# Four PSUM banks in turn for the pieces of a visit, and smaller steps for the work between

## The chip, the cores and the metric

The kernel runs on one core of a Trainium2 chip. The metric is device time in microseconds for one execution, from the median of ten runs. Everything is in float32.

## The reference

The input x has two images of 256 channels and 56 x 56 places, so 3136 tokens an image. The first layer is a linear attention over places (a convolution of 1 x 1 on each side, batch normalisation, relu, and x added). The second layer works on tokens:

```
t = to_tokens(x)                                   # (2, 3136, 256)
t = t + softmax_causal(q k^T / 8) v @ W_proj       # 4 heads of 64, on layernorm(t)
# mixture of experts, on n = layernorm(t):
probs = softmax(n @ gate_w + gate_b)               # 8 experts
cw    = the two largest probs of a token, else 0
t = t + sum_e cw[:, e] * (gelu(n @ W1[e] + b1[e]) @ W2[e] + b2[e])
```

W1 is 256 x 512 for each expert, W2 512 x 256. The kernel computes only the two chosen experts of a token, so each image's tokens have to be sorted by expert before the experts can start on them.

## The kernel before, in words

**Stages.** The first layer takes the first 100 us. Then comes the attention of image ("batch") 0, then of batch 1, from about 108 to 868 us, then the experts, in 105 blocks of 128 rows, 3.73 us of TensorE a block. Batch 0 is sorted while batch 1's attention runs, batch 1 while the first 42 blocks of the experts run, which hold batch 0's rows alone.

**Attention.** `attend` (L631) goes through seven tiles i of 448 queries. For each tile and each pair of heads hp (two), it goes through the key chunks j of 128: 4, 7, 11, 14, 18, 21 and 25 of them, so 200 steps a batch. A step is `scores` (L668, four 64 x 64 quadrants of TensorE at once, into a tile of two PSUM banks), the exponential on ACT (L676), for the chunks that the diagonal cuts a mask on DVE (L678), and the row sums on DVE (L690). `values` (L708) follows three steps later (`LAG`, L777). A key chunk is whole when no query of the tile is ahead of it, and cut otherwise; each pair of heads has four or five cut chunks, which alternate with whole ones at the end of its steps.

**PSUM.** All eight banks are in use: pool `pm` (L465) has two single banks, `psc` (L1869) two tiles of two banks for the scores, `py` one tile of two banks for the values. `bank` (L469) hands out those of `pm`. Every piece of work between the steps takes its bank from there: the projections of queries and keys (`query_key`, L550, copied out by ACT at L558), of values (`value`, L565, copied at L574), the transposes of normalised tokens (L536, copied at L542), the output projection (`project_out`, L618, added by DVE at L623), and the sums over keys (`sum_rows`, L732, copied at L737).

**Visits.** After the last step of a pair of heads comes a `visit` (L1913), 28 in all. It issues the projections that a later tile needs (`ahead`, L1875): four pieces for queries and keys or values, and one or two transposes; the last visits of batch 0 do this for batch 1, and in the last tile of batch 1 there are none. Then `sum_rows` runs. Between the steps, `between` (L1924) is called once for each step.

**The queue.** Other work lies in generators in a `queue`: `tokens(b)` (L1784), which runs `project_out`, then `dispatch`, and for batch 0 the loads of W1 (`w1s`) and of the first expert rows (`early_rows`). A generator gives True when a portion is done, False when it has to wait, and "pe" when TensorE work is next. `pull(n)` (L1757) goes through the queue from its front until n portions are done; a generator that gave False lets the next one have its turn, one that gave True ends the search. One that gave "pe" is held until `products` (L1772), called twice in a visit, lets it go on. Before the change, `between` calls `pull(2)` at every second step, and each visit calls `pull()` twice:

```python
                        for _ in range(2):
                            pull()
                            products()
```

`project_out` (L608) works in pairs of token chunks: for each chunk the product over two halves of 128 channels into one bank, the addition, for batch 0 a store to `rest_d`, and then for the pair the mean and variance of each chunk (`stats`, L173: `bn_stats` L177 and `bn_aggr` L178). After that it gives True once for batch 0, three times for batch 1.

**Sorting.** `dispatch` (L951) computes the inverse deviation of all tokens with four Newton steps on DVE, the gate's softmax, the two experts and the place of each token; nearly all are DVE operations on 25 to 200 elements a partition. Behind most of them stands `yield from op()`, which for batch 0 gives True once or twice in turn. At its end the rows are scattered: for each of the 25 chunks DVE writes a normalised copy `xr` (L1302) and POOL issues two indirect DMAs to `x_slots` (L1310). For batch 0 the copies take turns in two buffers, and a chunk gives True and then False.

**Experts.** At block n the program first fetches the rows of three blocks (one group) up to n + 6 ahead on SP (`fetch`, L1332, DMA L1350), loads groups up to n + 3 (`load`, L1368), then does the products of block n, the transposes of blocks n + 1 or n + 2, and `meanwhile` (L1997), which pulls two portions of the queue, three while batch 1 is being sorted. Group 14 is the first with rows of batch 1. Its fetch at block 36 calls `need` (L1977), which pulls until all of batch 1's rows have been sent:

```python
                def need(b):
                    while not sent[b]:
                        pull(every=True)
```

SP runs its queue in order, so the stores of results (L1466) that come after a fetch wait behind it.

The engines' instruction order is the program's order in these stages.

Of the kernel before, what the change touches and what calls it, by code (L numbers as in the profile page):

```python
# [10 lines left out]
F32 = mybir.dt.float32  # L11
# [17 lines left out]
def conv_attn_moe_kernel(  # L29
# [52 lines left out]
    P = 128  # L82
# [9 lines left out]
    NCH = -(-N // P)  # L92
    W = 448
# [79 lines left out]
    def stats(b, n, m, k, pool, nm):  # L173

        for a in range(m):
            st6 = pool.tile([P, 6], F32, tag="st6", name=f"st6_{nm}_{n}_{a}")
            nc.vector.bn_stats(st6[:k], ts[b][:k, n + a, :C])  # L177
            nc.vector.bn_aggr(ts[b][:k, n + a, MEAN : MEAN + 2], st6[:k])  # L178
# [9 lines left out]
    with tc.tile_pool(name="c_w", bufs=1) as cw, tc.tile_pool(name="c_s", bufs=2) as cs, tc.tile_pool(  # L188
        name="c_big", bufs=5, space=PSUM
# [169 lines left out]
        first = fold(0, gram(0, iter(())))  # L359
# [99 lines left out]
    def layer1(nm, general):  # L459

        with ExitStack() as whole:
# [4 lines left out]
            bg = pool(whole, "bg", bufs=2)  # L466
            g1 = pool(whole, "g1", bufs=1)

            def bank(name, shape=(P, 512)):  # L469
                return pm.tile(list(shape), F32, tag="m", name=f"{name}_{nm}")  # L470

            def centre_gate(place):
# [135 lines left out]
            def project_out(b, qT, done):  # L608

                for first, m, k in pairs():  # L610
                    while done() < (first + m - 1) * P + k:
                        yield False
                    yield "pe"
                    for n in range(first, first + m):
                        o = n * P
                        ps = bank(f"pp_{b}_{n}")
                        for c in range(NH):
                            nc.tensor.matmul(  # L618
                                ps[:k, : C + E], qT[:, c, o : o + k], wpr[:, c, :],
                                start=(c == 0), stop=(c == NH - 1),  # L620
                            )
                        t = ts[b][:k, n, : C + E]
                        nc.vector.tensor_tensor(t, t, ps[:k, : C + E], ALU.add)  # L623
                        if b == 0:
                            nc.sync.dma_start(out=rest_d[:k, n], in_=t[:, :C])
                    stats(b, first, m, k, bg, f"o{nm}{b}")

                    for _ in range(3 if b else 1):
                        yield True

            def attend(  # L631
                b, qT, kT, v, fst, fs, psc, py, visit, between, clock, later, finished
# [4 lines left out]
                steps, firsts = [], {}  # L637
                for i in range(NB):
                    nk = -(-((i + 1) * W) // P)
                    whole_js = [j for j in range(nk) if (j + 1) * P - 1 <= i * W]  # L640
                    cut = [j for j in range(nk) if j not in whole_js]
# [136 lines left out]
                for n in range(len(steps) + LAG):  # L778
                    if 0 < n <= len(steps) and steps[n - 1][4]:
                        i, hp = steps[n - 1][:2]  # L780
                        visit(i, hp)
                        sum_rows(hp, i)
                    if n < len(steps):
                        i = steps[n][0]
                        between(i, ends[i] - n)

                    late = n >= LAG and steps[n - LAG][3]
                    if n >= LAG:
                        due(clock[0])
                        clock[0] += 1  # L790
                    if n >= LAG and not late:
                        values(n - LAG)
                    if n < len(steps):
                        scores(n)
                    if late:
                        values(n - LAG)
# [154 lines left out]
            def dispatch(b):  # L951

                t = ts[b]
                tail = chunk(NCH - 1)
                ops = [0]

                def small_piece():

                    if b:
                        yield True  # L960
# [5 lines left out]

                def op():

                    ops[0] += 1
                    for _ in range(0 if b else 1 + ops[0] % 2):  # L970
                        yield True

                def small(name, last=E, dt=F32):
# [2 lines left out]
                def wide(ap):  # L976
# [8 lines left out]
                    small(k, 1).rearrange("p t o -> p (t o)") for k in ("newton_x", "newton_y", "red")  # L985
                )
                nc.vector.tensor_scalar(x, var, 1e-5, None, ALU.add)
                nc.vector.tensor_scalar(
                    y.bitcast(I32), x.bitcast(I32), 1, None, ALU.arith_shift_right
                )  # L990
                nc.vector.tensor_scalar(
                    y.bitcast(I32), y.bitcast(I32), -1.0, float(0x5F3759DF), ALU.mult, ALU.add
                )
                yield from small_piece()
                for i in range(4):
                    to = var if i == 3 else y
                    nc.vector.tensor_tensor(z, y, y, ALU.mult)
                    nc.vector.tensor_tensor(z, z, x, ALU.mult)
                    nc.vector.tensor_scalar(z, z, -0.5, 1.5, ALU.mult, ALU.add)
                    nc.vector.tensor_tensor(to, y, z, ALU.mult)  # L1000
                    yield from op()
                    yield from small_piece()
# [294 lines left out]
                for n in range(NCH):  # L1297
                    kk = chunk(n)
                    xr = (scatter_rows[0] if b else bg).tile(
                        [P, width], F32, tag="xr", name=f"xr_{nm}{b}_{n}"  # L1300
                    )
                    nc.vector.tensor_scalar(  # L1302
                        xr[:kk, :C], t[:kk, n, :C],
                        t[:kk, n, MEAN : MEAN + 1], t[:kk, n, RSTD : RSTD + 1],
                        ALU.subtract, ALU.mult,
                    )
                    if b:
                        nc.vector.tensor_copy(xr[:kk, C:], t[:kk, n, C + E - 2 : SLOT + 1])  # L1308
                    for k in range(2):
                        s = nc.gpsimd.indirect_dma_start(  # L1310
                            out=xds[b],
                            out_offset=bass.IndirectOffsetOnAxis(ap=idxs[b][:kk, k, n : n + 1], axis=0),
                            in_=xr[:kk],
                            in_offset=None,
                            bounds_check=xds[b].shape[0] - 1,
                            oob_is_err=False,
                        )
                        group = f"x_slots_{nm}{b}"
                        tc.declare_no_dep(s.ins, group=group, reason="different rows")
                        tc.add_to_no_dep_group(group, s.ins)  # L1320
                        if b or k:
                            yield True
                    if b == 0:
                        yield False
                sent[b] = True

            def experts(w1s, w2s, b2s, ex, es, ps6, between, need, written, settle, decide):
# [538 lines left out]
            else:  # L1866
                fst = pool(att, "fst", bufs=5)
                fs = pool(end, "fs", bufs=2, side="right")
                psc = pool(att, "psc", bufs=2, space=PSUM)  # L1869
                py = pool(att, "py", bufs=1, space=PSUM)  # L1870
                projections = [project_qkv(b, qT, kT, v, px) for b in range(B)]
                finished = [[0] * NH for b in range(B)]
# [2 lines left out]
                def ahead(b, i, hp):  # L1875

                    xs, qks, vs = projections[b]
                    if i + 1 < NS:
                        if hp == 0:
                            return qks(i + 1), xs(i + 2)[:1]  # L1880
                        return vs(i + 1), xs(i + 2)[1:]
                    if b + 1 == B:
                        return [], []
                    xs, qks, vs = projections[b + 1]
                    if hp == 0:
                        return [], xs(0)
                    return qks(0) + vs(0), xs(1)
# [22 lines left out]
                for b in range(B):  # L1910
                    queue.append(tokens(b, qT, lambda b=b: min(finished[b])))

                    def visit(i, hp):  # L1913

                        now, then = ahead(b, i, hp)
                        for piece in now:
                            piece()
                        for _ in range(2):
                            pull()
                            products()  # L1920
                        for piece in then:
                            piece()

                    def between(i, left):  # L1924
                        if b == B - 1 and i == NB - 1:

                            now = load_w2(left < NCH - 4)
                            for _ in range(1 if left > NCH - 4 else 2):
                                next(now, None)

                        tick[0] += 1
                        if tick[0] % 2:
                            pull(2)

                    due = attend(
                        b, qT, kT, v, fst, fs, psc, py, visit, between,
                        clock, later, finished[b],
                    )
# [250 lines left out]
```

## Time and profile before

| | |
|---|---|
| median of 10 runs | 1320.39 us (1318.14 to 1324.05) |
| the profiled execution | 1321.51 us, span 1319.8 us |
| matmuls of scores (L668), 3184 records | 339.4 us busy |
| matmuls of values (L708), 3184 records | 339.9 us busy |
| exponentials (L676), 400 | 331.0 us on ACT |
| row sums (L690), 372 | 379.9 us on DVE |
| first hidden product of the experts (L1432) | 205.8 us busy in all 102 blocks |
| DMA | 124.49 MB, mean 94 GB/s |

Busy time of an engine is the time in which at least one of its instructions ran. Matmuls are pipelined and their ends are modelled. In the waits, a row names the engine, the tile that the waiting instruction writes and its line, then what released it, then the total in us, how often, and the longest. In the timeline a row is the start, the length, the engine, the line and the operation; the brackets hold the idle time before it and what ended that.

### The profile page before, as it was taken

The page shows a single profiled execution, that of the slowest core. Times are in us where ns is not written, and L with a number is a line of the kernel's source. Part 1 is how long each engine was busy: PE and PEld are TensorE (multiplying, and loading weights), DVE is VectorE, ACT ScalarE, POOL GpSimd, SP SyncE. Part 2 cuts the span into 40 slices and gives each one's busy share as a digit, 9 for nine tenths or more (in the row PEclk, how much of TensorE's full clock was granted, in tenths as well). Part 3 has the DMA queues.
Part 4 walks back from the last instruction along what each step waited for, and adds up shares of the span by engine and source line. Part 5 has one row for each costly group of instructions (what it writes and reads, how often), then busy time and mean ns, then how long its engine had stood idle before and what let it go on. Part 6 is the DMA issues. An engine that isn't in the chain of part 4 may idle for free. (4 is left out here: it accounts for less than half of the span.)

```text
span 1319.8 us, 28094 instructions
## 1 busy us (share of the span) xinstructions
PE 1268.9 (96%) x10589; PEld 825.6 (63%) x10589; DVE 796.0 (60%) x1665; ACT 610.6 (46%) x1228; POOL 347.7 (26%) x317
## 2 busy tenths in 40 slices
PE   8999999999999999999999999999998999899997
PEld 7875445544444445444444444579987899799996
DVE  1582667567777744766877777764753443355654
ACT  0154565555666554555555556543422333234432
POOL 1103330000002223310116630000066312655551
PEclk9999999999999999999999999999999999899999
DMA  9994100000000001000002233321234333466654
GB/s 306 384 349 133 31 11 30 24 9 25 9 16 9 25 1 26 23 16 9 14 18 81 81 140 96 104 73 54 68 129 146 118 113 98 139 190 193 196 158 128
DMA packets 111182, 124.49 MB, mean 94 GB/s; under 512 B 19686, under 2 KB 100823, under 8 KB 111040
## 3 DMA queue, kind: packets, MB, share of 16 engines
q1 hardware_dynamic: 97216, 93.44, 23.2%
q0 software_dynamic: 9840, 25.67, 5.8%
q10 hardware_dynamic: 3984, 3.50, 0.9%
q8 instruction: 87, 1.43, 0.5%
q14 instruction: 55, 0.45, 0.1%
HBM read 62.71 MB, written 61.05 MB: 94 GB/s over the span
## 5 line engine op out<-in xcount | busy, mean ns | idle before, releaser
L676 ACT ACTIVATE st_f<-sc_f 128x896 f32<-128x896 f32 (+5 forms) x400 | 331.0, 841 | 222.7 <-PE sc_f L668 194.5
L690 DVE TENSOR_TENSOR acc_f<-acc_f,st_f 128x896 f32<-128x896 f32 (+5 forms) x372 | 379.9, 1021 | 71.3 <-ACT st_f L676 59.8
L668 PE MATMUL sc_f<-qT_f,kT_f 64*64 64x448 f32 (+6 forms) x3184 | 339.4, 500 | 6.4 <-ACT st_f L676 3.4
L708 PE MATMUL yp_f<-st_f,v_f 64*64 64x448 f32 (+6 forms) x3184 | 339.9, 501 | 5.3 <-DVE st_f L678 4.2
L1441 ACT ACTIVATE g_f<-ht_f,b1b 128x128 f32<-128x128 f32 x408 | 117.0, 372 | 251.9 <-PE ht_f L1432 137.4
L668 PEld LDWEIGHTS sc_f<-qT_f,kT_f 64*64 64x64 f32 x3184 | 119.3, 133 | 162.3 <-issue 124.4
L708 PEld LDWEIGHTS yp_f<-st_f,v_f 64*64 64x64 f32 x3184 | 117.9, 133 | 159.3 <-issue 134.0
L1432 PE MATMUL ht_f<-xT_f,w_f 128*128 128x128 f32 x1632 | 205.8, 279 | 6.4 <-issue 5.3
L1432 PEld LDWEIGHTS ht_f<-xT_f,w_f 128*128 128x128 f32 x1632 | 201.4, 195 | 13.2 <-issue 7.9
L720 POOL TENSOR_TENSOR qT_f<-both_f 128x448 f32<-128x448 f32 x28 | 36.9, 1318 | 502.3 <-ACT both_f L719 502.3
L1310 POOL DMA_INDIRECT x_slots<-xr_f,idx x100 | 110.0, 1100 | 142.8 <-DVE xr_f L1308 98.9
L1420 DVE COPY w_f<-w1s_f 128x1024 f32 x102 | 72.2, 710 | 91.5 <-PE ht_f L1432 40.3
L521 POOL TENSOR_SCALAR xn_f<-t 128x256 f32<-128x256 f32 (+1 forms) x50 | 80.9, 1626 | 158.5 <-PE xp_f L536 66.2
L1472 POOL DMA_INDIRECT y_tokens<-ys_f,to_f x57 | 57.8, 1015 | 126.8 <-DVE ys_f L1461 103.1
L550 PE MATMUL qk_f<-px_f,wat 128*128 128x512 f32 (+2 forms) x224 | 88.3, 546 | 0.4 <-ACT px_f L542 0.4
L1461 DVE TENSOR_TENSOR ys_f<-yp_f,kT_f 128x128 f32<-128x128 f32 x102 | 29.6, 290 | 96.5 <-PE yp_f L1451 71.7
L550 PEld LDWEIGHTS qk_f<-px_f,wat 128*128 128x128 f32 x224 | 40.5, 190 | 45.6 <-issue 41.1
L686 DVE COPY acc_f<-st_f 128x896 f32<-128x896 f32 x28 | 17.9, 641 | 79.9 <-ACT st_f L676 76.1
L1451 PE MATMUL yp_f<-px_f,g_f 128*128 x204 | 62.6, 387 | 3.1 <-issue 3.1
L1451 PE MATMUL yp_f<-v_f,g_f 128*128 x204 | 62.0, 384 | 2.3 <-issue 2.3
L678 DVE TENSOR_TENSOR st_f<-st_f,keep 128x256 f32<-128x256 f32 (+1 forms) x112 | 45.7, 408 | 29.7 <-ACT st_f L676 29.7
L1451 PE MATMUL yp_f<-kT_f,g_f 128*128 x204 | 62.1, 385 | 0.9 <-issue 0.6
(274 smaller groups left out, 1269.3 us busy)
## 6 DMA issues: line engine op xcount, KB each, us to landing
x_slots<-fill SPq DMA_DIRECT2D x1, 8190.0 KB
xb_f<-x_slots SPq DMA_DIRECT2D x60, 130.0 KB
x_slots<-fill SPq DMA_DIRECT2D x1, 7296.0 KB
y_slots<-ys_f SPq DMA_DIRECT2D x57, 128.0 KB
kept<-t SPq DMA_DIRECT2D x2, 3200.0 KB
x<-in_x_dram SPq DMA_DIRECT2D x14, 448.0 KB
rb_f<-inverses SPq DMA_DIRECT2D x56, 112.0 KB
xr<-in_x_rows_dram SPq DMA_DIRECT2D x12, 512.0 KB
```

The source lines that it names most:

```text
L521: nc.gpsimd.tensor_scalar(xn[:k, a], ts[b][:k, n + a, :C], ts[b][:k, n + a, MEAN : MEAN + 1], ts[b][:k, n + a, RSTD : RSTD + 1], ALU.subtr ...
L550: nc.tensor.matmul(ps[:, :w], wat[:, c, d0 : d0 + P], px[:, s % 2, c, :w], start=(c == 0), stop=(c == NH - 1),)
L668: nc.tensor.matmul(ps[h : h + HS, a, c0:W], kT[hp][rows, j * P + h : j * P + h + HS], qT[rows, hp, q0 + c0 : q0 + W], start=True, stop=True,)
L676: nc.scalar.activation(st[:k, :, c0:], ps[:k, :, c0:W], AF.Exp, scale=SCALE)
L690: nc.vector.tensor_tensor(acc[:k, :, c0:], acc[:k, :, c0:], st[:k, :, c0:], ALU.add)
L708: nc.tensor.matmul(yp[a * HS : (a + 1) * HS, h // HS, c0:W], v[hp][h : h + HS, j, a, :HS], st[h : h + HS, a, c0:], start=first, stop=bool( ...
L1310: s = nc.gpsimd.indirect_dma_start(out=xds[b], out_offset=bass.IndirectOffsetOnAxis(ap=idxs[b][:kk, k, n : n + 1], axis=0), in_=xr[:kk], i ...
L1420: nc.vector.tensor_copy(w, w1s[:, :, bass.ds(e, 1), :].rearrange("p c e h -> p c (e h)"))
L1432: nc.tensor.matmul(ht[:, k, :], w[:, c, k * P : (k + 1) * P], xT[:, c, :], start=(c == 0), stop=(c == NH - 1),)
L1441: nc.scalar.activation(g[:, k, :], ht[:, k, :], AF.Gelu, bias=b1bs[b][:, k, i : i + 1])
L1451: nc.tensor.matmul(yp[:, :C], g[:, k, :], w2s[k][:, bass.ds(e, 1), :].rearrange("p e d -> p (e d)"), start=(k == 0), stop=(k == KH - 1),)
L1472: s = nc.gpsimd.indirect_dma_start(out=y_tokens, out_offset=bass.IndirectOffsetOnAxis(ap=to[:, n % GB : n % GB + 1], axis=0), in_=ys, in_o ...
```

## The change

The change has four parts.

1. During a visit `bank` goes round four places: the two banks of `pm`, then the two halves of a tile of `psc`, taken as a score tile would be. A new score tile is taken at every third place of the round. `sum_rows` after the visit, and work pulled in `between`, use `pm` alone, as before.
2. For batch 0 `project_out` no longer computes the variances in the visit. It puts a generator `closer` at the front of the queue, which does one chunk a portion, and goes straight on to the next pair. `dispatch` of batch 0 starts when all 25 are closed.
3. For batch 0 every operation of the sorting, those of the Newton steps too, is now a portion of its own (`op` gives True once), and a scattered chunk gives True twice instead of True and False.
4. Visits do not pull any more. `between` pulls one portion at each step, except at the cut steps of the first tile, which has no others.

```diff
+            ring, score_banks = [], []
+
             def bank(name, shape=(P, 512)):
+                turn = ring[0] % 4 if ring else 0
+                if turn > 1:
+                    if turn == 2:
+                        ring[1] = score_banks[0].tile([P, 2, 512], F32, tag="sc", name=f"{name}_{nm}")
+                    ring[0] += 1
+                    flat = ring[1][:, turn - 2]
+                    if shape[2:]:
+                        return flat[:, : shape[1] * shape[2]].rearrange("p (a w) -> p a w", a=shape[1])
+                    return flat[:, : shape[1]]
+                if ring:
+                    ring[0] += 1
                 return pm.tile(list(shape), F32, tag="m", name=f"{name}_{nm}")
...
                         if b == 0:
                             nc.sync.dma_start(out=rest_d[:k, n], in_=t[:, :C])
+                    if b == 0:
+                        queue.appendleft(closer(b, first, m, k))
+                        continue
                     stats(b, first, m, k, bg, f"o{nm}{b}")
 
-                    for _ in range(3 if b else 1):
+                    for _ in range(3):
                         yield True
+                while b == 0 and unclosed[0]:
+                    yield False
+
+            unclosed = [NCH]
+
+            def closer(b, first, m, k):
+
+                for n in range(first, first + m):
+                    stats(b, n, 1, k, bg, f"o{nm}{b}")
+                    unclosed[0] -= 1
+                    yield True
...
-                        between(i, ends[i] - n)
+                        between(i, ends[i] - n, (steps[n][2] + 1) * P > i * W + 1)
...
                 def op():
 
-                    ops[0] += 1
-                    for _ in range(0 if b else 1 + ops[0] % 2):
+                    if b == 0:
                         yield True
...
                 for i in range(4):
                     to = var if i == 3 else y
                     nc.vector.tensor_tensor(z, y, y, ALU.mult)
+                    yield from op()
                     nc.vector.tensor_tensor(z, z, x, ALU.mult)
+                    yield from op()
                     nc.vector.tensor_scalar(z, z, -0.5, 1.5, ALU.mult, ALU.add)
+                    yield from op()
                     nc.vector.tensor_tensor(to, y, z, ALU.mult)
                     yield from op()
...
                     if b == 0:
-                        yield False
+                        yield True
                 sent[b] = True
...
                 psc = pool(att, "psc", bufs=2, space=PSUM)
+                score_banks.append(psc)
...
                         now, then = ahead(b, i, hp)
+                        ring[:] = [0, None]
                         for piece in now:
                             piece()
                         for _ in range(2):
-                            pull()
                             products()
                         for piece in then:
                             piece()
-
-                    def between(i, left):
+                        ring.clear()
+
+                    def between(i, left, cut):
...
                         tick[0] += 1
-                        if tick[0] % 2:
-                            pull(2)
+                        if not cut or i:
+                            pull()
```

Three more `yield from op()` stand behind the three operations ahead of the Newton loop.

More of the change, by code (lines that the diff above doesn't have):

```diff
@@ L954, in dispatch @@
                 tail = chunk(NCH - 1)
-                ops = [0]
                 def small_piece():
@@ L997, in dispatch @@
                     nc.vector.tensor_tensor(z, y, y, ALU.mult)
+                    yield from op()
                     nc.vector.tensor_tensor(z, z, x, ALU.mult)
+                    yield from op()
                     nc.vector.tensor_scalar(z, z, -0.5, 1.5, ALU.mult, ALU.add)
+                    yield from op()
                     nc.vector.tensor_tensor(to, y, z, ALU.mult)
```

## The prediction

> **What bounds the kernel now.** I read the busy shares and the clock row first, then busy time by stretches of the span, then the waits of TensorE inside the attention, then two rows of the timeline.
>
> ```profile
> PE 1268.9 (96%) x10589; PEld 825.6 (63%) x10589; DVE 796.0 (60%) x1665; ACT 610.6 (46%) x1228; POOL 347.7 (26%) x317
> ```
>
> TensorE is busy 96% of the span, and the other engines hang on it. A change can only give back its gaps, so the question is in which stretch they lie and what ends them. By stretches (columns: length, then busy time of PE, PEld, DVE, ACT, POOL, granted clock, DMA share, GB/s):
>
> ```profile
> 108.00:545.00 437.00, 430.06 (x4093) 205.98 (x4094) 279.61 (x422) 242.29 (x377) 81.13 (x52) 1.00 0.08 20
> 545.00:685.00 140.00, 134.96 (x1322) 62.05 (x1325) 101.25 (x192) 78.68 (x119) 20.52 (x13) 1.00 0.05 10
> 685.00:775.00 90.00, 82.95 (x842) 35.97 (x844) 67.55 (x103) 45.43 (x63) 60.82 (x52) 1.00 0.28 92
> ```
>
> These three are nearly the whole attention: up to 545 plain attention, 545 to 685 with the first batch's sorting between its steps, 685 to 775 with its scatter. PE is idle for 6.9, 5.0 and 7.1 us. The expert stage splits at the second batch's scatter:
>
> ```profile
> 868.00:956.00 88.00, 86.69 (x585) 79.82 (x582) 52.04 (x163) 35.14 (x112) 1.36 (x1) 1.00 0.24 72
> 956.00:1040.00 84.00, 74.17 (x458) 66.17 (x456) 37.79 (x148) 23.80 (x85) 51.48 (x50) 0.94 0.39 128
> ```
>
> From 956 to 1040 POOL issues 50 indirect DMAs, PE is idle 9.8 us and the clock falls to 0.94. What PE waited for in the attention (108 to 870):
>
> ```profile
> PE yp_f L708 <- DVE st_f L678: 4.2, 7, 1.1
> PE sc_f L668 <- ACT st_f L676: 3.4, 5, 1.2
> PE xp_f L536 <- DVE t L623: 2.2, 6, 1.1
> PE sp_f L732 <- DVE t L623: 1.9, 3, 0.7
> PE sp_f L732 <- ACT kT_f L558: 1.8, 7, 0.4
> ...
> PE sp_f L732 <- ACT v_f L574: 0.9, 3, 0.3
> ...
> PE pp_f L618 <- DVE t L623: 0.6, 1, 0.6
> ```
>
> Each sp, xp and pp row is a visit's piece that wants one of two PSUM banks whose last reader, a copy on ACT or an add on DVE, is not done: the wait that four banks should remove. The first two rows are the steps' own chain, in which the sorting's operations stand on DVE. Last, when batch 1's rows are out: the final scatter and the first fetch behind it on SP.
>
> ```profile
> 1036.03 1.12 POOL L1310 DMA_INDIRECT x_slots<-xr_f,idx  x1 [0.30 <-issue]
> ```
> ```profile
> 1038.95 1.44 SPq L1350 DMA_DIRECT2D xb_f<-x_slots  x3
> ```
>
> **The banks.** A visit with four pieces, a transpose and sum_rows asks for six banks. Of two, sum_rows takes the one that the last-but-one piece has just filled. Of four, it takes one filled five pieces earlier. The rows above plus ACT px 0.4 and DVE L585 0.2 are 5.2 us for sp, 2.2 for xp and 0.6 for pp: 8.0. Of these the two visits of batch 1's last tile stay: there one pair takes turns 0 and 1 and sum_rows comes back to turn 0, 0.57 us each. That leaves 6.9. The upper end is the weight loads' idle time before the same instructions: 16.2 us at L732 (6.2, 5.2, 3.4, 1.2, 0.2), and about 4 at L536 and L618, so 20; part of it lies under matmuls that still stream. I take 8, near PE's own rows. New waits, with the other pieces, the scores and so ACT's exponentials queued behind them on PE: the first borrowed bank, third in a visit, must be left by the exponential two steps back; in the visit at 431 it was left as the visit began (431.47), two bank times of 0.89 before it is wanted. The second borrowed pair is wanted at the seventh bank, 5 us on. Scores after the visit wait for copies of 0.59 us, emptied several pieces earlier except where the transpose itself is the borrowed one: 0 to 3 us, taken at 0. Its cover is the score buffer's idleness in a visit; without it each of 28 visits would pay one 0.59 copy, 16 us.
>
> **The variances.** 25 chunks of 0.41 (L177) plus 0.18 (L178) are 14.8 us of DVE, moved out of the visits, one chunk per step. A full step is 1.5 us of PE and 1.09 of DVE (L690), so a 0.59 is 0.18 too much for it; four in a row lag 0.7 us, which five st buffers cover and later steps recover. Price 0. In the short tiles (7 to 11 steps) the cover may fail: 0.7 in 6 visits, 4 us. The rest_d stores keep their place on SP.
>
> **The sorting.** Yields of batch 0's dispatch: before, 42 op() calls at 1.5 each plus 20 others, 83; after, 57 plus 20, 77. But pulls fall too: before, one per step on average and two in each visit; now one per step and none in visits. I walked both step lists: its first operation moves from visit i=1, hp=1 of batch 1 to step 23, its first scatter from step 94 to 100, its last from 138 to 148 (of 200). The w1 loads follow at 150 to 164 and the first expert rows at 166 to 169, behind nothing on SP but that scatter and ahead of step 200 by 30 steps, 45 us: hidden. Past POOL's queue the scatter moves beside one more sum L720 of 1.3 us. DVE no longer meets Newton in bursts of four, and no extra chunk falls into a visit, where DVE stood 5.4 us for L1302 on the two xr buffers. PE's idle rows here are 2.3 (545 to 685, L678) and 5.8 (685 to 775: sc 2.2, yp 1.9, sc issue 1.7). I take 2 of these 8.1 as gained. Ends: 5 gained; or 4 lost, since at a tile's end eight steps with masks need about 9.4 us of PE and 8.7 of DVE, and eight operations of 0.3 instead of five make DVE late by 0.8 in five tiles.
>
> **What the order does to batch 1.** While dispatch always yields True, and the scatter now too, tokens(1) behind it in the queue is never reached. Before, the scatter's False let it through: pairs 2, 4 and 6 of its projection ran in visits at 709, 750 and 788. Now these three wait, 3 x 1.78 = 5.3 us of PE (a pair is eight records of L618, 0.222 apart), which leave the attention and come back in the experts: zero in sum. Behind them its sorting starts at block 17 instead of 12, its scatter at block 25 instead of 20. Block 36 forces what is left, since fetch(14) needs all rows: one chunk of 25 before, eight now. DVE takes 8 x 0.58 = 4.6 us of it, within the two blocks by which weights run ahead. POOL is the bound: 0.98 plus 0.30 idle is 1.28 per DMA, 62.7 us from first to last, 76.8 in this trace because of gaps. Five blocks of 3.73 move the first from 959.26 to 977.9 (without the stalls, which fall later then). The end is 1040.6 at full rate, 1054.7 with all the old gaps, and 1046 with two gaps of 2.8, which I take. SP then issues 2.9 later, as above; behind it stand the y_slots stores of blocks 33 on. From SP's issue to block 42's transposes at 1049.50 were 10.6, of which I take 5 as slack: the addition L1386 (0.96) ran at 1045.07 behind other DVE work, and only 5.6 are needed. So the transposes come at 1049, 1055 or 1063: 0, 5 or 14 us lost. A gain is excluded, since the same POOL work starts later. I take 5.
>
> The stalls of this stretch went with a clock of 0.94. [...]
>
> **Sum.** The profiled execution took 1321.51 us (span 1319.8), 1.1 over the median of 1320.39. 1321.5 - 8 (banks) - 2 (sorting) + 5 (batch 1) = 1316.5, and 1315.4 against the median. I forecast 1315.5. Own range: bank gain 7 to 12, sorting -5 to +2, batch 1 0 to 9, which together rarely reach their ends: 1307 to 1321.
>
> **The rivals.**
> - *Slower: the second batch's scatter decides.* Place: SP's fetch L1350 at block 36, with PE idle at block 40. Price 14 for the late rows, and 5 for a slow clock as from 1137 to 1160 (23 us at 0.78, 0.22 x 23), less 10 gained: 1329. It decides once the last scatter comes 15 us later than now. For it: POOL is fed only 1.5 chunks a block; against: at full rate it ends within 5 us of before.
> - *DVE takes the waits over.* Gain 6 at the banks, 4 lost at the masks, 4 at batch 1: 1322. For it: L678 is already the longest wait; against: DVE is busy 72% from 545 to 685.
> - *Everything hides.* Banks 14, sorting 4, batch 1 nothing: 1302.
> - *The change doesn't do what it says.* If a borrowed tile's halves are waited for together, the second half waits for the copy of the first, 0.59 plus 0.2, in some 24 visits: 19 lost, no bank gain, 1342. No row shows a tile used so.
>
> **How the numbers follow.** Forecast 0.58, scatter 0.16, DVE 0.14, hides 0.08, not as said 0.04. About 0.2%, 2.6 us, is what a measurement here can tell from no change. Of the forecast 0.52 is faster by more and 0.06 within; hides is faster; DVE gives 0.02 faster, 0.09 same, 0.03 slower; scatter 0.02 same and 0.14 slower. Faster 0.62, same 0.17, slower 0.21. The range leaves out the last case, most of hides and the tail of scatter: 1304 to 1328.
>
> **What would show it.** Right: rows of sp, xp and pp on L558, L574 and L623 nearly gone in the attention; clock 1.00 there; the attention ends some 15 us earlier (10 gained, 5 of moved matmuls); batch 1's first scatter near 968 (977.9 less 10) instead of 959; SP's L1350 behind it and a PE gap at block 40. Wrong: new waits of PE on L558 or L574 at pieces or scores, more than 10 us on L678, or no gap at block 40.

## The result and the profile after

The changed kernel takes 1351.12 us (median of 9 runs, 1347.71 to 1354.62) beside 1320.75 for the kernel before (31 runs, 1314.83 to 1324.87). The ratio is 1.0232, 95% interval 1.0216 to 1.0248: 30 us slower, where 5 us faster was forecast, and beyond the range's upper end of 1328. The profiled execution took 1347.96 us, its span is 1346.2, so 26.4 us over the span of before. The change adds lines, so those of after lie higher: matmuls of queries and keys L563 (L550 before), of values L578 (L565), their copies L571 and L587 (L558, L574), the second batch's scatter L1341 (L1310), the fetch behind it L1381 (L1350), the expert blocks' transposes L1440 (L1409).

The page first. TensorE is busy about as long as before (1271.7 us, 1268.9 before), in a longer span:

```profile
PE 1271.7 (94%) x10589; PEld 823.4 (61%) x10589; DVE 792.1 (59%) x1665; ACT 607.7 (45%) x1228; POOL 352.5 (26%) x317
```

The stretches of the span (columns as in the table of before) say where:

```profile
108.00:545.00 437.00, 420.88 (x3983) 198.68 (x3985) 267.88 (x400) 234.03 (x363) 76.14 (x49) 1.00 0.08 20
545.00:685.00 140.00, 135.54 (x1342) 62.36 (x1334) 101.07 (x195) 78.52 (x123) 24.91 (x15) 1.00 0.05 12
685.00:775.00 90.00, 84.05 (x840) 36.92 (x840) 64.06 (x96) 48.08 (x69) 45.05 (x37) 1.00 0.17 55
...
1000.00:1100.00 100.00, 75.69 (x483) 67.44 (x482) 38.60 (x142) 25.23 (x90) 47.24 (x46) 0.88 0.38 119
```

Up to 545, TensorE is now idle for 16.1 us instead of 6.9, in the plain attention where the banks were to help. In 545 to 775 the idle time is 10.4 instead of 12.1. And from 1000 to 1100 it is idle 24.3 us at a clock of 0.88.

**First loss: the attention.** The first expert block starts at 880.14 us instead of 869.65, although three pairs of projections, 5.3 us of TensorE, left the attention. What TensorE waited for from 108 to 871 (us in total, times, longest):

```profile
PE qk_f L563 <- ACT kT_f L571: 8.8, 13, 1.2
PE v_f L578 <- ACT v_f L587: 4.8, 9, 0.5
PE sc_f L695 <- ACT st_f L703: 4.0, 5, 1.2
PE pp_f L631 <- DVE t L636: 2.6, 5, 0.5
PE v_f L549 <- ACT v_f L587: 2.2, 2, 1.6
...
PE yp_f L735 <- DVE st_f L705: 0.4, 1, 0.4
```

Against the waits of before, the rows of qk_f and v_f are new (the one at L549 is a transpose into the second half). The old ones did shrink: the rows of sp_f add up to 2.5 instead of 5.2, and the first row of before, values behind the mask on VectorE (L678, now L705), fell from 4.2 to 0.4. What the new rows are is seen in the first visit (timeline: start, duration, engine, line and operation; in brackets the idle time before it and what ended it):

```profile
113.03 5.42 PE L563 MATMUL qk_f<-px_f,wat 128*128 128x512 f32 x12
...
118.48 0.58 ACT L571 COPY kT_f<-qk_f 128x512 f32<-128x512 f32 x1 [1.13 <-PE qk_f L563]
...
119.12 1.98 PE L563 MATMUL qk_f<-px_f,wat 128*128 128x512 f32 x4 [0.68 <-ACT kT_f L571]
```

Three pieces run on without a gap: twelve matmuls. The third is the first half of the borrowed tile. ScalarE copies it from 118.48 to 119.06, and only then do the four matmuls of the fourth piece start, which write the other half.

**Second loss: block 40.** The rows of the second batch come too late. The wait of TensorE from 975 to 1084, and the way to it:

```profile
PE tp_f L1440 <- DVE xb_f L1417: 19.9, 1, 19.9
```

```profile
1066.12 0.91 POOL L1341 DMA_INDIRECT x_slots<-xr_f,idx  x1 [0.31 <-issue]
1069.40 1.02 SPq L1381 DMA_DIRECT2D xb_f<-x_slots  x3
...
1074.74 0.96 DVE L1417 TENSOR_TENSOR xb_f<-xb_f,xo_f 128x768 f32<-128x768 f32 x1 [1.94 <-DMA y_slots<-ys_f]
...
1075.81 0.45 PE L1440 MATMUL tp_f<-ident,xb_f 128*128 128x128 f32 x1 [19.92 <-DVE xb_f L1417]
```

The last scatter is issued at 1066.12, 30 us later than in before, the fetch behind it on SP at 1069.40, the addition of VectorE at 1074.74, and then the transposes for which TensorE has stood since 1055.9. (The addition's bracket names a store, of which SP issued three from 1071.00 on. The addition waits for the fetch at L1393 too, and the row does not tell which came last.) So 9.7 us pass from the last scatter to the transposes. In before it was 13.5, from 1036.03 to

```profile
1049.51 0.38 PE L1409 MATMUL tp_f<-ident,xb_f 128*128 128x128 f32 x2
```

without a wait of TensorE there. The granted clock is 1.00 from 1057 to 1059, 0.84 from 1059 to 1060, and then 0.50:

```profile
1060.00:1070.00 10.00, 0.00 (x0) 0.00 (x0) 0.00 (x0) 1.14 (x4) 5.50 (x6) 0.50 0.26 83
1070.00:1080.00 10.00, 4.19 (x12) 3.51 (x13) 3.14 (x9) 0.37 (x1) 0.00 (x0) 0.50 0.75 209
```

Counted from its first hidden product to that of block 41, block 40 takes 25.73 us instead of 3.73: 19.92 of waiting, and 2.1 more of working at half clock.

### The profile page after: what moved, and what is told of

Same layout as the page of the kernel before. It is cut to its first block, busy times and chain, and to the rows that moved or that the text cites. A ratio compares the mean times of both kernels' runs of the same rounds, so it can differ in the third digit from the quotient of the medians.

```text
span 1346.2 us, 28031 instructions
## 1 busy us (share of the span) xinstructions
PE 1271.7 (94%) x10589; PEld 823.4 (61%) x10589; DVE 792.1 (59%) x1665; ACT 607.7 (45%) x1228; POOL 352.5 (26%) x317
## 4 chain that ended last, share of the span: by engine, by line
PE 86%; issue 4%; DVE 3%; ACT 3%; DMA 2%; POOL 1%; SPq 0%; DVEq 0%; POOLq 0%; ACTq 0%
PE yp_f L735 19%; PE sc_f L695 19%; PE ht_f L1463 12%; PE yp_f L1482 11%; PE qk_f L563 7%; PE v_f L578 4%; PE pp_f L631 3%; PE cp L339 3%; PE gram L270 3%; PE tp_f L1440 2%; POOL x_slots L1341 1%; ACT st_f L703 1%; DVE acc_f L717 1%; PE sp_f L759 1%; PE yo_f L1705 1%
## 5 line engine op out<-in xcount | busy, mean ns | idle before, releaser
L1463 PE MATMUL ht_f<-xT_f,w_f 128*128 128x128 f32 x1632 | 202.8, 277 | 4.0 <-issue 2.7
L1463 PEld LDWEIGHTS ht_f<-xT_f,w_f 128*128 128x128 f32 x1632 | 198.2, 193 | 10.9 <-issue 5.6
L1341 POOL DMA_INDIRECT x_slots<-xr_f,idx x100 | 113.0, 1130 | 172.7 <-DVE xr_f L1339 116.6
L563 PE MATMUL qk_f<-px_f,wat 128*128 128x512 f32 (+2 forms) x224 | 91.7, 552 | 9.1 <-ACT kT_f L571 8.8
L563 PEld LDWEIGHTS qk_f<-px_f,wat 128*128 128x128 f32 x224 | 39.6, 189 | 58.8 <-issue 36.8
L705 DVE TENSOR_TENSOR st_f<-st_f,keep 128x256 f32<-128x256 f32 (+1 forms) x112 | 45.9, 410 | 33.1 <-ACT st_f L703 31.1
L1482 PE MATMUL yp_f<-w2s_f,g_f 128*128 x204 | 62.1, 386 | 0.2
```

Of the source, the lines that this page charges most:

```text
L563: nc.tensor.matmul(ps[:, :w], wat[:, c, d0 : d0 + P], px[:, s % 2, c, :w], start=(c == 0), stop=(c == NH - 1),)
L1341: s = nc.gpsimd.indirect_dma_start(out=xds[b], out_offset=bass.IndirectOffsetOnAxis(ap=idxs[b][:kk, k, n : n + 1], axis=0), in_=xr[:kk], i ...
L1463: nc.tensor.matmul(ht[:, k, :], w[:, c, k * P : (k + 1) * P], xT[:, c, :], start=(c == 0), stop=(c == NH - 1),)
L1482: nc.tensor.matmul(yp[:, :C], g[:, k, :], w2s[k][:, bass.ds(e, 1), :].rearrange("p e d -> p (e d)"), start=(k == 0), stop=(k == KH - 1),)
```

## The experiments

Two theories were tested. **Halves:** the program orders the two halves of a borrowed tile as one tile, so the second half waits for the first half's copy. **Queue:** with the scatter of the first batch yielding True, the second batch's sorting starts later, and its last rows set the end of block 40. Each kernel ran beside the kernel before on the same chip. On the three chips of the experiments the kernel before took a median of 1319.76, 1325.2 and 1325.4 us, so only ratios are compared; 1% is 13.2 us of 1320.75. In the table, "first block" is the start of the first hidden product in the expert stage, the scatter's times count from there, "to block 41" from the last scatter to that block's first hidden product, "experts" from the first block to the end of the span. All from one profiled execution each.

| kernel | ratio (95%) | first block | scatter first, last | to block 41 | experts |
|---|---|---|---|---|---|
| before | 1 | 869.7 | 89.6, 166.4 | 15.4 | 450.1 |
| after | 1.0232 (1.0216-1.0248) | 880.1 | 113.1, 186.0 | 13.6 | 466.0 |
| own_tiles | 1.0065 (1.0048-1.0082) | 855.9 | 115.1, 189.1 | 13.7 | 472.6 |
| let_through | 1.0134 (1.0102-1.0165) | 888.7 | 93.2, 170.4 | 11.3 | 450.7 |
| own_and_let | 0.9912 (0.9885-0.9939) | 859.2 | 93.1, 171.8 | 12.9 | 456.6 |
| before_shut | 1.0103 (1.0066-1.0140) | 866.0 | 112.9, 187.3 | 13.3 | 468.7 |
| own_alone | 0.9938 (0.9916-0.9961) | 863.7 | 89.9, 166.2 | 17.7 | 453.5 |
| halves_alone | 1.0160 (1.0133-1.0187) | 893.2 | 89.8, 166.4 | 17.8 | 455.6 |
| steps_alone | 0.9982 (0.9964-1.0000) | 870.5 | 93.2, 171.0 | 12.0 | 454.8 |
| faster_pull | 1.0101 (1.0067-1.0136) | 859.9 | 87.9, 160.5 | 40.1 | 480.5 |
| halves_free | 1.0034 (1.0017-1.0050) | 853.0 | 113.5, 187.1 | 13.3 | 467.6 |
| free_and_let | 0.9924 (0.9904-0.9944) | 857.5 | 93.9, 172.2 | 11.0 | 449.0 |

**own_tiles.** After, with two score tiles in place of one tile's halves:

```diff
-                    if turn == 2:
-                        ring[1] = score_banks[0].tile([P, 2, 512], F32, tag="sc", name=f"{name}_{nm}")
                     ring[0] += 1
-                    flat = ring[1][:, turn - 2]
+                    flat = score_banks[0].tile([P, 2, 512], F32, tag="sc", name=f"{name}_{nm}")[:, 0]
```

Expected:

> The kernel after, but each borrowed bank is a score tile of its own (its first half), instead of the two halves of one tile. Theory A (the two halves are ordered as one tile, so the piece in the second half starts only when the copy of the first half is done; 13 + 9 such waits of 0.5 to 0.7 us in the trace of after, and more on the scores behind them): the rows qk_f <- kT_f and v_f <- v_f inside the attention fall from 13.6 us to under 4, the first expert block comes 12 to 18 us earlier than at 880 us, and the time falls to 1332 to 1338; the wait of 20 us at block 40 stays. Rival (ACT is simply late, because the copies now run beside exponentials that want the same score buffers): the waits move to the scores, the first expert block comes less than 4 us earlier, and the time stays above 1346.

Measured: 1.0065 instead of 1.0232, 22 us. The first block comes 24.3 us earlier, more than expected. Its waits of TensorE from 108 to 871 begin with

```profile
PE sc_f L693 <- ACT st_f L701: 7.1, 9, 1.3
```

No row of qk_f or of v_f is left. The 24.3 are complete: from 108 to the first block TensorE's idle time fell from 31.9 to 15.0, and its busy time from 740.3 to 732.9. Part of a wait is counted as busy: the sixteen matmuls of the first visit above make 5.42 and 1.98, together 7.40, and 7.13 where they run in one row, as in halves_free below. The scores' wait did grow, from 4.0 to 7.1, as the rival had it, but by 3 us, not by 24.

The stall before block 41 stayed, as expected, but not as one row. Blocks 37 to 39 take 8.2, 18.1 and 5.0 us, 20 too much, and among TensorE's waits from 957 to 1060 are

```profile
PE ht_f L1461 <- issue: 6.4, 8, 1.3
PE yp_f L1480 <- issue: 6.4, 7, 1.8
...
PE tp_f L1438 <- issue: 2.0, 2, 1.1
```

waits for nothing that the profile shows. They are taken up below.

**let_through.** After, with the queue as before:

```diff
                     if b == 0:
-                        yield True
+                        yield False
                 sent[b] = True
```

Expected:

> The kernel after, but a scattered chunk of the first batch lets the queue go on to the second batch's tokens, as in the kernel before. Theory B (the second batch's sorting is held back behind the first batch's scatter, starts five blocks later and its last rows come too late for block 40): the first scatter of the second batch comes again within 2 us of five blocks earlier (18 us) than in after relative to the first block, the wait at block 40 (19.9 us) is gone or below 3, the clock stays above 0.9 there, and the time falls by 15 to 20, to 1331 to 1336. Rival (the wait at block 40 is made by something else that the change moved, the stores or the weights on SP): a wait of over 10 us stays and the time is above 1343.

Measured: 1.0134, 13 us off. Expected was 15 to 20, so a little less came; block 40 now takes 4.4 us. The scatter of the second batch by its line (50 DMAs: shortest, median and longest in ns, first and last start in us), in before, in after and here:

```profile
L1310 POOL DMA_INDIRECT x_slots<-xr_f,idx x50: 914/977/1557, 959.3 to 1036.0; - x50
```
```profile
L1341 POOL DMA_INDIRECT x_slots<-xr_f,idx x50: 909/972/1864, 993.2 to 1066.1; - x50
```
```profile
L1341 POOL DMA_INDIRECT x_slots<-xr_f,idx x50: 912/974/1557, 981.9 to 1059.1; - x50
```

From the first block it starts 89.6, 113.1 and 93.2 us on, and it takes 73 to 77 us in all three: what is lost at its start is still lost at its end.

**own_and_let.** Both edits. Expected:

> Both edits at once: a tile of its own for each borrowed bank, and the first batch's scattered chunk lets the second batch's tokens go on. If A and B are the two causes and add up: 1351 less 15 less 18 = 1318, 1311 to 1322, with the bank waits of before gone as well. If the two share one cause, or the sorting's one operation a step costs by itself (the rival of VectorE being late for the masks, priced at 6 to 8): 1325 or more.

Measured: 0.9912, faster than before by 11.6 us, more than expected. With both losses mended the change is a gain. Mended one at a time they give 22 and 13 us, mended together 42. The four intervals reach 2 to 4 us to each side, so part of the 7 us between the sum and the 42 can be noise; that the mends help each other is not excluded.

**before_shut.** The kernel before, with `yield True` for the `yield False` of let_through's diff. Expected:

> The kernel before, with one word changed: a scattered chunk of the first batch no longer lets the queue go on. Theory B alone: the first scatter of the second batch comes four blocks later (15 us), the last one as late as in after, and there is a new wait of 10 to 20 us near block 40, 1330 to 1341. If the scatter's end has slack, as the prediction took it (0, 5 or 14 lost): 1320 to 1326.

Measured: 1.0103, 13.6 us slower, from one word. The scatter starts 23 us later after the first block (15 expected) and ends 21 later, and the experts take 18.6 us more. Part of it comes back in the attention, which three pairs have left: the first block comes 3.7 us earlier.

**own_alone and halves_alone.** The kernel before with the banks alone, once with tiles of their own and once with the change's halves, the queue, the variances and the sorting as before (here the ring is set aside while a visit pulls from the queue):

```diff
                         now, then = ahead(b, i, hp)
+                        ring[:] = [0, None]
...
                         for _ in range(2):
+                            state = ring[:]
+                            ring.clear()
                             pull()
+                            ring[:] = state
                             products()
...
+                        ring.clear()
```

Expected:

> The kernel before with the banks alone: pieces and transposes of a visit take four banks in turn, each borrowed one a score tile of its own; its queue, its variances and its sorting stay as in before. Bank term of the prediction (8 of the rows sp, xp and pp): the first expert block comes 6 to 12 us earlier than in before, the rows sp_f fall from 5.2 to about 2, and the time falls by 6 to 12, ratio 0.991 to 0.996. Rival (the gain in the attention of the run with own tiles came from the moved pairs and the calmer sorting, not from banks): less than 3 us earlier, ratio above 0.998.

> The kernel before with the banks alone as the change has them: the two borrowed banks are the two halves of one score tile. If the order between the halves is the whole cost, the difference to the run with own tiles alone is that of after to own_tiles, 22 us: 10 to 16 us slower than before, ratio 1.008 to 1.012, with rows of qk_f and v_f that wait for the copies on ScalarE, 12 to 18 us in sum. If the halves cost only together with the variances as later pieces and the sorting at one operation a step: less than 5 us slower, ratio below 1.004.

Measured: 0.9938 with own tiles, 8.2 us gained, and the first block comes 6.0 us earlier; 1.0160 with halves, 21 us lost, where 10 to 16 were expected. Their waits of TensorE in the attention, own tiles first:

```profile
PE sc_f L679 <- ACT st_f L687: 6.2, 9, 1.4
...
PE sp_f L743 <- DVE t L634: 2.4, 3, 1.3
```
```profile
PE qk_f L563 <- ACT kT_f L571: 7.6, 12, 0.7
PE pp_f L631 <- DVE t L636: 6.1, 6, 1.4
PE sc_f L681 <- ACT st_f L689: 5.3, 7, 1.9
PE v_f L578 <- ACT v_f L587: 4.8, 9, 0.5
```

The only difference between the two is whether a visit's third and fourth bank belong to one tile, and so whether they take one score buffer or two (that this does not explain the loss is shown by halves_free below). It is worth 29 us. TensorE from 108 to the first block, own tiles first:

```profile
108.00:863.65 755.65, 738.76 (x7233) 349.89 (x7232) 520.53 (x813) 418.45 (x628) 166.48 (x120) 1.00 0.13 36
108.00:893.20 785.20, 746.89 (x7244) 353.03 (x7242) 521.13 (x815) 419.81 (x633) 164.99 (x120) 1.00 0.12 36
```

It is idle for 38.3 us with halves and for 16.9 with own tiles. It is also not only ScalarE's copies: the second of two products waits for VectorE's addition to the first (pp_f, 6.1).

**steps_alone.** The variances as later pieces, one sorting operation a step and no pull in a visit, with two banks and the queue let through. It is own_and_let without `ring[:] = [0, None]`. Expected:

> The kernel before with the variances as later pieces, the sorting one operation a step and no pull in a visit, but two banks as before and the queue let through after a scattered chunk of the first batch. The prediction's terms: variances 0, sorting 2 gained, so 0 to 5 us faster than before, ratio 0.996 to 1.000. Rival (VectorE late for the masks, or at the short tiles): 2 to 8 us slower, ratio 1.0015 to 1.006, with more than 8 us on the rows yp_f <- st_f and sc_f <- st_f.

Measured: 0.9982 with an interval that reaches 1.0000, 2.4 us: the prediction's 2, at the edge of what can be told from nothing. TensorE's idle time from 545 to 775 fell from 12.1 to 9.7, where the prediction looked for it. But in the attention as a whole the steps' waits only changed their place: behind the masks (yp_f) they fell from 4.2 to 0.3, behind the exponentials (sc_f) they rose from 3.4 to 7.9. Their sum, 8.2, is over the rival's sign of 8, without the rival's loss.

**faster_pull.** own_and_let with four pulls a block in place of three:

```diff
-                    pull(3 if sorting or worked[0] >= MIXED else 2, every=True)
+                    pull(4 if sorting or worked[0] >= MIXED else 2, every=True)
```

Expected:

> Both mended parts (a tile of its own for each borrowed bank, the queue let through), and four pulls instead of three per expert block while the second batch is sorted and scattered. Theory: the last scatter sets when block 41 starts (11 to 15 us later in all kernels so far), so an earlier last scatter is worth something: the first scatter comes some 7 us earlier relative to the first block, the last one 5 to 10, the stall at block 40 is gone, and the time is 3 to 8 us below that of both mends alone (ratio to before 0.985 to 0.989). Rival (GpSimd's DMAs are the bound, or VectorE, with more work per block, becomes late): no gain or a loss, ratio to before 0.991 or above.

Measured: 1.0101, a miss. The scatter ended 11 us earlier, and block 40 took 3.73, as the theory had it. But the expert stage took 24 us more than in own_and_let. Its longest blocks are 16 (8.4 us), 23 (8.4), 24 (8.1), 29 (11.4) and 31 (13.5). The waits after 871 begin with

```profile
PE gdp_f L1769 <- DVE judge_f L1765: 9.5, 1, 9.5
PE yp_f L1480 <- issue: 8.7, 15, 1.5
PE ht_f L1461 <- issue: 8.7, 12, 1.1
PE rank_f L1098 <- DVE both_f L1087: 3.8, 1, 3.8
```

Two of these rows are the pulled work's own small matmuls, which wait on VectorE with the block's products behind them. The rate of three pulls was worth keeping. That the last scatter decides holds only while nothing else is made late.

**halves_free and free_and_let.** Is it the program's order or the chip? After, still with one tile's halves, but each matmul into the second half is declared independent of the instructions that read the first. The data are disjoint. In the second kernel the queue is let through as well.

```diff
+            def filled(turn, *writers):
+                for w in writers if turn == 3 else ():
+                    for r in readers:
+                        tc.declare_no_dep(w.ins, r, reason="different halves")
...
-                        nc.tensor.matmul(
+                        filled(turn, nc.tensor.matmul(
...
-                    nc.scalar.copy(to[:, first:end], ps[:, :w])
+                    left(turn, nc.scalar.copy(to[:, first:end], ps[:, :w]))
```

Expected:

> The kernel after, with the two borrowed banks still the halves of one score tile, but declared independent of each other: a matmul into the second half no longer waits for the copy or the addition that reads the first half. If the wait is made by the order that the program keeps between accesses to one tile, this is worth what tiles of their own are worth (21 to 23 us off the ratio of after, 1.023 to 1.006): ratio 1.003 to 1.010, the rows of qk_f and v_f on the copies under 3 us, the first expert block at 854 to 862. If the cost lies in the chip (TensorE writing one bank while ScalarE reads the neighbouring one) or in the number of score buffers that a visit takes: above 1.015.

> The same with the queue let through after a scattered chunk of the first batch: both causes mended in the change's own layout. Expected as both mends with tiles of their own: ratio 0.988 to 0.994. If one score buffer for two borrowed banks, instead of two, is worth something to the scores behind a visit: another 1 to 4 us below that. If the halves cost in the chip: 1.000 or above.

Measured: 1.0034 and 0.9924, both as expected for an order that only the program keeps; the first block, at 853.0, is 1 us earlier than expected. Whether a visit takes one score buffer or two is not settled: 0.9924 against the 0.9912 of own_and_let is no difference, 1.0034 against the 1.0065 of own_tiles is 4 us for one buffer, with intervals that just touch. The first visit of halves_free, TensorE and then ScalarE:

```profile
112.62 7.13 PE L577 MATMUL qk_f<-px_f,wat 128*128 128x512 f32 x16
```
```profile
118.07 0.59 ACT L585 COPY kT_f<-qk_f 128x512 f32<-128x512 f32 x1 [1.13 <-PE qk_f L577]
```

All sixteen matmuls run on without a gap, 1.78 a piece, while ScalarE copies the third piece beside the fourth, in the time that a copy takes while TensorE stands (0.58 in after).

In halves_free the stall at block 40 is one row again:

```profile
PE tp_f L1457 <- DVE xb_f L1434: 19.7, 1, 19.7
```

In free_and_let, whose only difference is the queue, the row is gone.

## Why the prediction was wrong, step by step

**The banks (8 gained): right in size, for another kernel.** With tiles of their own the banks alone are worth 8.2 us, ratio 0.9938, an interval from 5 to 11 us. That it is 8 again is partly luck. The rows of sp_f, xp_f and pp_f fell by 4.6, from 8.0 to 3.4, and the scores' wait on the exponentials rose from 3.4 to 6.2, within the 0 to 3 that the prediction had named for it and taken at 0. The first block came 6.0 us earlier.

The failed step is the last part on the banks: the new waits were taken at 0, on the cover that a score buffer is idle in a visit. That cover is about a buffer and its last reader. It says nothing about two pieces that share one tile, and there the waits cost 22 us (after against own_tiles) to 29 (halves_alone against own_alone). The case stood among the rivals as "the change doesn't do what it says", with the right mechanism and the right place. Its price was close too: 19 lost and no bank gain, where halves_alone lost 21. Only its chance was wrong, 0.04, for the reason that no row showed a tile used so. That is a reason for not knowing, not for 4 in 100; the diff showed both pieces taken from one tile.

**The variances (0) and the sorting (2 gained): not contradicted.** Together they measured 0.9982, 2.4 us, with an interval that reaches 1.0000. The idle time fell where it was looked for, while the rows show a wait that moved from the masks to the exponentials.

**The order of batch 1 (5 lost): right in mechanism and place, wrong in size.** It cost 13.6 us in before_shut, 13 between after and let_through, 14.5 between halves_free and free_and_let and 20 between own_tiles and own_and_let. The step's top was 14. It failed in its first two terms; the third, the slack, was nearly right.
- The start was put five blocks of 3.73 later, 18.7. It came 23.5 later after the first block. The three moved pairs, "zero in sum" for TensorE, stand ahead of the sorting and are not zero for the start of the scatter: before has five blocks of 5.51 us there, after has eight, and 18.7 and 3 x 1.78 make 24.0.
- The end was put 10 later, by taking two gaps of 2.8 for the old gaps. It came 19.6 later: the scatter took 72.9 us instead of 76.8, so of the 14 us of gaps over the full rate of 62.7 some 10 stayed. Of the step's own cases this is the third, "all the old gaps".
- The slack was taken as 5. From the last scatter to the transposes behind it were 13.5 us in before. In after, halves_free and before_shut, where they start 0.1 us after the addition ends, it is 9.4 to 9.7 us. So the slack was about 4.

With the end 19.6 later and 3.8 of slack the transposes come 15.8 us late; the expert stage of after takes 15.9 more than that of before.

**The clock was a small term.** The sum has none for it; the rival of the scatter put 5 us beside 14 for the late rows. TensorE stood from 1055.9, the stretch from 1060 on shows 0.50, and the cost was 2.1 us at block 40, beside a wait of 19.92. The 22 waits at banks in after (qk_f at L563 and v_f at L578, up to 1.2 us) left the clock at 1.00 from 108 to the first block.

**The chances.** The two slower cases were priced one at a time, 1329 and 1342, as if only one could come true. They sit in different stages, and they nearly add up: halves alone lost 21.1, the queue alone 13.6, variances and sorting gained 2.4, together 32.3 us, and the change measured 30.6. The range of 1304 to 1328 left out the case of the halves altogether.

**What stays open.** In own_tiles and before_shut the stall ahead of block 41 is not one wait but a trickle: TensorE's "issue" rows are 14.8 and 17.3 us there, against 2.0 in after, 3.6 in halves_free and 2.9 in free_and_let. Before has 8.6 us of it, let_through 6.8, own_and_let 9.8, and faster_pull 9.9 from 935 to 1060. All of them send the same 50 scatter DMAs. One piece of it can be told: the longest "issue" waits of before_shut and own_and_let (2.8 and 3.2) stand before the transposes, which start 0.1 us after VectorE's addition ends. They are the wait for the last scatter under another name, so even with the queue let through the last scatter can hold TensorE up. No run tells what the rest waits for. In own_tiles it decides: the transposes start 11.8 us after the last scatter, 2.2 after the addition has ended.

## What to carry to other kernels

Before a buffer is split between two uses, ask what the unit of its order is. If two halves of one tile are tracked together, the second bank is a wait and not a bank. A tile for each turned 21 us lost into 8 gained, and in the whole change a declared independence did as well as tiles of their own. In a queue of generators the value that a step yields decides who runs next, so a one-word change is costed by walking the queue to the last consumer, with everything that now stands ahead of it. And where two risks lie in different stages, both can come true, and the range has to hold their sum.

## What the runs showed of the hardware

- TensorE wrote one bank of a borrowed tile while ScalarE read the other, and neither took longer for it: 16 matmuls took 7.13 us in halves_free, as with tiles of their own in own_tiles, and the copy beside them 0.59, where it took 0.58 in after with TensorE standing.
- In after TensorE stood from 1055.9, and its granted clock was 1.00 from 1057 to 1059, 0.84 from 1059 to 1060 and 0.50 from 1060. It stayed at 0.50 while TensorE worked again from 1075.8 to 1080; the stretch from 1080 to 1086 is back at 0.99.
- GpSimd's indirect DMAs of the second batch's scatter keep a median of 0.97 to 0.98 us, with a median of 0.30 between two of them, in all kernels; the longer gaps (0.55 to 3.33 us in halves_free) stand between two chunks.
- In own_tiles TensorE stalled for nothing that the profile shows from 957 to 1060, the stretch in which the scatter is issued: 17 times, by up to 1.8 us, 14.8 in sum.
